# A routed filter-and-experts kernel: whole tiles of one pair of experts, and lists of single experts for the tokens left over

## The chip, the cores and the metric

The kernel runs on one core of one Trainium2 chip. A core has five engines that run side by side, each with its own queue of instructions, and wait for one another through semaphores: TensorE (PE, matrix products, whose loads of stationary operands are listed as PEld), VectorE (DVE), ScalarE (ACT), GpSimd (POOL) and SyncE (SP). Transfers between the chip's memory (DRAM) and the on-chip memory (SBUF) are issued by SP, ACT or POOL and carried out by 16 DMA engines. Products of PE land in PSUM, from where DVE or ACT read them.

The metric is the device time of one execution in microseconds. Differences of the median of several executions are looked at.

## The reference

The input is 16 x 1024 = 16384 tokens of 512 numbers (E = H = 512), with 8 experts, each a 512 x 512 matrix in float32. Every token goes to the two experts with the largest router probabilities.

```python
xn = _layernorm(x)
# s: a filter in frequency, then 24 bits per token, corrected, times W_le
x1 = ifft(fft(xn) * filt).real
bits = (sigmoid(x1 @ W_el + b_el) > 0.5)
s = x1 + _golay_correct(bits) @ W_le + b_le
# g: two of eight experts
probs = softmax(xn @ router_w.T)
topk_vals, topk_idx = top_k(probs, 2)
topk_w = topk_vals / (topk_vals.sum(-1) + 1e-6)
out = ((expert_out[topk_idx] + topk_vals) * topk_w).sum()   # over the two
g = silu(out)
return x + s * g
```

Here `expert_out` is `xn` times the matrix of each expert. The term `topk_vals` is a number per token and choice that is added to every element of that expert's result.

## The kernel before

A tile is 128 tokens; there are NT = 128 of them. The kernel has two passes, both with an order of instructions written out by hand (`tc.manual_schedule()`), so each engine runs its queue just as the Python loops emit it.

**Pass one** (`pass_1`) goes over the tokens in the order of memory. For each tile it computes the filter as matrix products and the logits of router and bits (`fold`, `transpose`, `filt`), stores the filtered values to DRAM (`yd`), and for rounds of tiles finds the two experts of every token (`route`). The two experts make one of 28 pairs. `scatter` writes the token's number into that pair's list in DRAM (`lists`), one indirect transfer of POOL per tile. `put_records` stores a record of 28 numbers per token (`recd`): in columns 0 to 7 the weights of the eight experts (six of them zero), in 9 the sum of weight times probability, in 10 and 11 mean and scale of the layer norm, and behind them the corrected bits.

At its end `bounds_a`, `bounds_b`, `place_q` and the four `takes` functions work out, from the counts of the pairs, where each of the 128 tiles of the second pass finds its tokens, and which experts it needs.

**Pass two** (from `mp = ctx.enter_context(...)`, L1026 on) goes over the tokens in the order of the lists. The pairs are put on a path (`pair_path`) on which neighbours share an expert, and the lists are read one behind the other along it, cut into 128 tiles with no regard to where a pair ends. A tile that lies in one pair needs two experts, and each of the 27 changes from pair to pair adds one more, so there are NI = 2 x 128 + 27 = 283 products of a tile with an expert. Which product belongs to which tile and expert depends on the data; it is read into registers (`load_regs`, L1110, four products at a time and four ahead), and the operands are addressed by these registers:

- `fetch_tok` (L1044) gathers 128 token numbers from the lists, `fetch_x` gathers their rows of x and their records, `fetch_y` their filtered values; `put` (L1186) scatters the results to the output. Every one of them is an indirect transfer of 128 rows, and all are issued on POOL's queue, in the order in which the loop calls them: five for each tile.
- `normalize` (DVE, L1079), `turn` (PE, L1087: four transposes into PSUM) and `enter` (ACT, L1093) bring a tile's normalized tokens, transposed, into a ring of 16 slots; `take` (ACT, L1124) copies the slot that a product needs.
- `product` (PE, L1135) multiplies with one expert: four steps over the inner size, eight instructions in the profile. DVE adds it, times the expert's column of weights, to the tile's sum (L1143). `open_tile` sets that sum to zero (L1099) and copies the eight weights (L1098).
- `triple`, `turn_code` (L1157, L1162, L1166) and `mend` (L1172, L1173) add the corrected bits' product to the filtered values; `gate` (ACT, L1150) is the silu; `combine` (DVE, L1177 to L1182) undoes the filter's halving, multiplies and adds x.

The loop runs over products `i`. Tile t = i / 2 is prefetched 8 (token numbers), 6 (x and records), 4 (normalized) and 2 (turned) tiles ahead, and is finished 14 tiles later, when all its products are sure to be done:

```python
for i in range(NI + 2 * LAST):
    t = i // 2
    f = t - LAST
...
    if i % 2 == 0:
        if 0 <= f - 1 < NT:
            put(f - 1)
        if t + AHEAD_R < NT:
            fetch_tok(t + AHEAD_R)
```

Five buffers of PSUM hold results of `product` and `mend`, two those of `turn`, one that of `turn_code`.

Of the kernel before, what the change touches and what calls it, by code (L numbers as in the profile page):

```python
# [21 lines left out]
RING = 16  # L22
# [5 lines left out]
def pair_path(ne=8):  # L28

    pairs = [(a, b) for a in range(ne) for b in range(a + 1, ne)]  # L30
    path, used = [(0, 1)], {(0, 1)}

    def go():
        if len(path) == len(pairs):
            return True
        for p in pairs:
            if p not in used and set(p) & set(path[-1]):
                path.append(p)
                used.add(p)
                if go():  # L40
                    return True
                path.pop()
                used.discard(p)
        return False

    assert go()
    return path
# [3 lines left out]
def kernel(  # L51
# [12 lines left out]
):  # L64

# [33 lines left out]
    NI = 2 * NT + NPAIR - 1  # L99
    NIP = (NI + 3) // 4 * 4  # L100

# [6 lines left out]
    yd = dram.tile([N, E], F32, name="yd")  # L108

# [21 lines left out]
    ones_b = p1c.tile([P, P], BF16, name="ones_b")  # L131
    iota_e = p1c.tile([P, NE], F32, name="iota_e")
# [3 lines left out]
    ord_sb = p1c.tile([NPAIR, 3 * NPAIR], F32, name="ord_sb")  # L136


    row_sb = p1c.tile([P, rows.shape[0]], F32, name="row_sb")
    base_r = row_sb[:, 0:NPAIR]  # L140
    dbase_r = row_sb[:, NPAIR : 2 * NPAIR]
    mem_r = row_sb[:, 2 * NPAIR : (2 + NE) * NPAIR].rearrange("p (e k) -> p e k", e=NE)
    at = (2 + NE) * NPAIR
    cnt_r = row_sb[:, at : at + 512]
    upto_r = row_sb[:, at + 512 : at + 512 + NE * NE].rearrange("p (a b) -> p a b", a=NE)
    bel_r = row_sb[:, at + 512 + NE * NE :]
# [66 lines left out]
    def constants():  # L213
# [19 lines left out]
        v.memset(wring, 0.0)  # L233
# [148 lines left out]
    def setup_code():  # L382
# [13 lines left out]
        for k in (1, 2):  # L396
# [15 lines left out]


            lambda: v.tensor_scalar(vi, vi, 16 * RING - 1, None, ALU.bitwise_and),
            lambda: v.tensor_scalar(ve, vi, -NONE, None, ALU.add),
# [22 lines left out]
    ti = mid.tile([P, 2], I32, name="ti")  # L438
    tf = mid.tile([P, 2], F32, name="tf")
    qi = mid.tile([P, NT], I32, name="qi")  # L440
    vi = mid.tile([P, NE], I32, name="vi")
    ve = mid.tile([P, NE], BF16, name="ve")
    NONE = 16.0 * ((NT - 1) % RING) + NE

# [198 lines left out]
    def route(n: int):  # L643
# [17 lines left out]
        def begin():  # L661
            s, j = t0 // GT, t0 % GT
            st.ex = (groups[s].wide if t0 < PAIRED else groups[s].ex)[:, j : j + S]
            st.rec = recs[(t0 // (2 * GT)) % 3][:, t0 % (2 * GT) : t0 % (2 * GT) + S, :]
            st.mx = new("mx", [P, S])
            v.tensor_reduce(st.mx, st.ex[:, :, L:X], AX.X, ALU.max)
# [11 lines left out]
        def largest(src, hot):  # L678
# [4 lines left out]
            def d():  # L683
                st.at = new("at", [P, S])
                v.tensor_reduce(st.at, st.eq, AX.X, ALU.max)
# [28 lines left out]
        def probs():  # L714
            st.sp = new("sp", SN)
            v.tensor_mul(st.sp, st.pb, st.sel)

        def norm_of():
            st.den = new("den", [P, S])
            v.tensor_reduce(st.den, st.sp, AX.X, ALU.add)  # L720

        ops += [chosen]
# [3 lines left out]
            lambda: v.tensor_mul(st.pb, st.pb, wide(st.sm)),  # L726
            probs,
            norm_of,
# [81 lines left out]
        def more():  # L810
            st.mo = small.tile([P, NPAIR], F32, name="mo", bufs=1)
            v.tensor_reduce(st.mo, st.q4.rearrange("p a k -> p k a"), AX.X, ALU.add)

        weights = [
            lambda: v.tensor_mul(st.rec[:, :, 0:NE], st.sp, wide(st.den)),
            lambda: v.tensor_mul(st.sp, st.sp, st.rec[:, :, 0:NE]),

            lambda: v.tensor_reduce(st.rec[:, :, 9], st.sp, AX.X, ALU.add),
# [17 lines left out]
    G = 16  # L836
    addrs = {}
    qf = bt.tile([P, NT], F32, name="qf")
    begin = bt.tile([P, NPAIR], F32, name="begin")
    step = bt.tile([P, NPAIR], F32, name="step")  # L840
    woff = bt.tile([1, NIP], I32, name="woff")
    slot = bt.tile([1, NIP], I32, name="slot")
    wcol = bt.tile([1, NIP], I32, name="wcol")
    wring = bt.tile([P, RING * 16], F32, name="wring")
    md = Group()

    def bounds_a():
        pc = ps_g.tile([P, 512], F32, name="pg")[0:NPAIR, 0:P]
        nc.tensor.matmul(pc, cum, ones_b, start=True, stop=True)
        md.cnt = mid.tile([NPAIR, P], F32, name="cntk")  # L850
        nc.vector.tensor_copy(md.cnt, pc)

    def bounds_b():

        po = ps_g.tile([P, 512], F32, name="pg")[:, 0 : 3 * NPAIR]
        nc.tensor.matmul(po, md.cnt, ord_sb, start=True, stop=True)
        nc.vector.tensor_copy(begin, po[:, 0:NPAIR])
        md.off = mid.tile([P, 2 * NPAIR], F32, name="off")
        nc.vector.tensor_copy(md.off, po[:, NPAIR:])
        nc.vector.tensor_sub(step, dbase_r, md.off[:, NPAIR:])  # L860

    def place_q(t: int, room):

        cmp = room[:, 0 : G * NPAIR].rearrange("p (g k) -> p g k", k=NPAIR)
        jump = room[:, G * NPAIR : G * (NPAIR + 1)]
        nc.vector.tensor_tensor(
            cmp,
            qf[:, t : t + G].unsqueeze(2).to_broadcast([P, G, NPAIR]),
            begin.unsqueeze(1).to_broadcast([P, G, NPAIR]),
            ALU.is_ge,  # L870
        )
        nc.vector.tensor_mul(cmp, cmp, step.unsqueeze(1).to_broadcast([P, G, NPAIR]))
        nc.vector.tensor_reduce(jump, cmp, AX.X, ALU.add)
        addrs[t // G] = bt.tile([P, G], I32, name="addr", bufs=2)
        nc.vector.tensor_add(addrs[t // G], jump, qf[:, t : t + G])

    def takes_a():

        end = md.off[:, 0:NPAIR]
        lo = mid.tile([P, NPAIR], F32, name="lo")  # L880
        nc.vector.tensor_scalar(lo, begin, tf[:, 0:1], None, ALU.max)
        hi = mid.tile([P, NPAIR], F32, name="hi")
        nc.vector.tensor_scalar(hi, end, tf[:, 1:2], None, ALU.min)
        nc.vector.tensor_tensor(lo, lo, hi, ALU.is_lt)
        use = mid.tile([P, NE, NPAIR], F32, name="use")
        nc.vector.tensor_mul(use, mem_r, lo.unsqueeze(1).to_broadcast([P, NE, NPAIR]))
        md.takes = mid.tile([P, NE], F32, name="takes")
        nc.vector.tensor_reduce(md.takes, use, AX.X, ALU.max)
        takes_b = mid.tile([P, NE], BF16, name="takes_b")
        nc.vector.tensor_copy(takes_b, md.takes)  # L890

        md.pn = ps_g.tile([P, 512], F32, name="pg")[:, 0:NE]
        nc.tensor.matmul(md.pn, tri_b, takes_b, start=True, stop=True)

    def takes_b():
        first = mid.tile([P, 1], F32, name="first")
        nc.vector.tensor_reduce(first, md.pn, AX.X, ALU.add)
        md.num = mid.tile([P, NE], F32, name="num")
        run = mid.tile([P, NE, NE], F32, name="run")
        nc.vector.tensor_mul(  # L900
            run, upto_r, md.takes.unsqueeze(1).to_broadcast([P, NE, NE])
        )
        nc.vector.tensor_reduce(md.num, run, AX.X, ALU.add)
        nc.vector.scalar_tensor_tensor(
            md.num, md.num, first, md.takes, ALU.add, ALU.mult
        )
        md.pi = ps_g.tile([P, 512], F32, name="pg")[0:1, 0:NIP]

    def takes_c(e: int):
        hot = mid.tile([P, NIP], BF16, name="hot", bufs=3)  # L910
        nc.vector.tensor_scalar(hot, cnt_r[:, 0:NIP], md.num[:, e : e + 1], None, ALU.is_equal)
        nc.tensor.matmul(md.pi, ve[:, e : e + 1], hot, start=(e == 0), stop=(e == NE - 1))

    def takes_d():
        nc.vector.tensor_scalar(wcol, md.pi, NONE, None, ALU.add)
        nc.vector.tensor_scalar(woff, wcol, NE - 1, None, ALU.bitwise_and)
        nc.vector.tensor_scalar(slot, wcol, 4, None, ALU.logical_shift_right)

    def pass_1():
# [23 lines left out]
        nc.gpsimd.iota(ti, pattern=[[P, 2]], base=0, channel_multiplier=P)  # L943
        nc.gpsimd.iota(vi, pattern=[[1, NE]], base=0, channel_multiplier=16)
        nc.gpsimd.iota(qi, pattern=[[P, NT]], base=0, channel_multiplier=1)
# [59 lines left out]
        bounds_a()  # L1005
        turn_a()
        bounds_b()
        turn_b()
        place_q(0, mid.tile([P, E], F32, name="cmp"))
        syndrome()  # L1010
        correct()
# [3 lines left out]
        takes_a()  # L1015
        takes_b()
        for e in range(NE):
            takes_c(e)
        takes_d()
# [6 lines left out]
    mp = ctx.enter_context(tc.tile_pool(name="mp", bufs=27))  # L1026
    xnp = ctx.enter_context(tc.tile_pool(name="xnp", bufs=3))
    xgp = ctx.enter_context(tc.tile_pool(name="xgp", bufs=22))
    w2 = ctx.enter_context(tc.tile_pool(name="w2", bufs=2))
# [73 lines left out]
    def load_regs(i: int):  # L1103
        for key, src, eng, top in (
# [12 lines left out]
            for n in range(4):  # L1117
                regs[key, i + n] = vals[n]
# [223 lines left out]
```

## Time and profile before

| | |
|---|---|
| median of 14 runs | 1552.24 us (1545.86 to 1562.89) |
| the profiled execution | 1555.33 us |
| its span | 1553.6 us |
| mean granted clock of PE | 0.962 |
| PE busy | 1425.9 us, 92% |
| DVE busy | 1144.2 us, 74% |
| POOL busy | 893.7 us, 58% |
| ACT busy | 627.3 us, 40% |
| instructions | 20646 |

The span is the time from the first to the last recorded instruction; the time of the execution holds a little more. The first pass takes some 370 us of it, the second the rest.

How to read the lines. A line of the page's groups gives the source line, the engine, the operation, what it writes and reads (`out<-in`), how often, and behind the bar the busy time in us, the mean of one in ns, and the idle time of the engine just before, with what ended it. In a line of the timeline come start and length in us, engine, line, operation, and in brackets the idle time before it and its releaser. "issue" means that the engine waited for nothing that the profile shows; "remote" or "an unknown queue" that a semaphore ended the wait for which the trace has no event in place. The ends of matmuls are modelled. In the slices each digit is the busy share of a fortieth of the span, in tenths.

### The profile page before, as it was taken

The numbers are of one execution on the slowest core, as the hardware profiler recorded it, in microseconds if no ns is written. First come the engines' busy times: TensorE is split into PE (matmuls) and PEld (weight loads), VectorE is DVE, ScalarE is ACT, GpSimd is POOL, SyncE is SP. The second block draws the span as 40 slices with busy tenths as digits, with TensorE's granted clock in tenths as the row PEclk, the third lists the DMA queues.
The fourth block names the chain that finished last, engine by engine and source line by source line (L and its number), as shares of the span: only waits on it lengthen the run. The fifth ranks groups of instructions, "written<-read, shape, count | busy, mean of one in ns | idle before, by whom it ended". The sixth has DMA issues, their size and how long they took to land.

```text
span 1553.6 us, 20646 instructions
## 1 busy us (share of the span) xinstructions
PE 1425.9 (92%) x5203; PEld 772.2 (50%) x5203; DVE 1144.2 (74%) x3043; ACT 627.3 (40%) x1346; POOL 893.7 (58%) x908
## 2 busy tenths in 40 slices
PE   3999999883999999898989889898999898999997
PEld 2888887672444444344434344344444343444443
DVE  7788888995343877777768677777787777779666
ACT  4988888761222332332323223233232323333221
POOL 1357777776544656666647456565756575564322
PEclk8999999995999999999999999999999999999999
DMA  6997766631111232233323222332333232232221
GB/s 230 318 333 259 223 224 224 161 100 52 51 43 54 94 97 90 91 96 104 99 81 107 80 90 90 96 98 90 110 97 97 90 111 90 90 97 96 76 74 61
DMA packets 91393, 185.07 MB, mean 119 GB/s; under 512 B 21998, under 2 KB 57710, under 8 KB 87182
## 3 DMA queue, kind: packets, MB, share of 16 engines
q0 software_dynamic: 43472, 104.51, 21.9%
q1 hardware_dynamic: 46702, 78.07, 15.0%
q10 hardware_dynamic: 1104, 1.17, 0.3%
q8 instruction: 46, 0.75, 0.2%
q14 instruction: 69, 0.57, 0.1%
HBM read 112.86 MB, written 70.84 MB: 118 GB/s over the span
## 4 chain that ended last, share of the span: by engine, by line
PE 56%; DVE 16%; issue 16%; another core or an unknown queue 5%; POOL 4%; ACT 1%; DMA 1%; DVEq 1%; POOLq 0%; ACTq 0%
PE pe L1135 36%; PE py L553 7%; PE pt L533 3%; PE pt L1087 2%; POOL yg L1044 2%; DVE aring L1143 2%; PE py L549 2%; PE py L550 1%; DVE mix L1181 1%; DVE yg L1173 1%; DVE aring L1099 1%; PE py L551 1%; PE pe L1172 1%; POOL rec L1044 1%
## 5 line engine op out<-in xcount | busy, mean ns | idle before, releaser
L1135 PE MATMUL pe<-w_sb,xw 128*128 x2264 | 1037.8, 608 | 3.1 <-issue 1.8
L1135 PEld LDWEIGHTS pe<-w_sb,xw 128*128 128x128 f32 x2264 | 419.9, 195 | 532.4 <-issue 509.8
L1143 DVE SCALAR_TENSOR_TENSOR aring<-pe,wring,aring 128x512 f32 x283 | 211.9, 749 | 275.9 <-remote 125.6
L1186 POOL DMA_INDIRECT out<-xg,tok x128 | 136.4, 1066 | 304.1 <-DVE xg L1182 195.2
L1150 ACT ACTIVATE aring<-aring,rec 128x512 f32<-128x512 f32 x128 | 92.4, 722 | 497.9 <-DVE aring L1143 378.5
L1124 ACT COPY xw<-xring 128x512 f32 x283 | 174.2, 617 | 29.1 <-PE pe L1135 21.5
L1044 POOL DMA_INDIRECT tok<-lists,at x120 | 124.7, 1039 | 88.1 <-DVE at L1060 55.4
L1044 POOL DMA_INDIRECT yg<-yd,tok x128 | 135.3, 1057 | 39.0 <-issue 39.0
L553 PE MATMUL py<-cm,pmt 128*128 128x288 f32 x512 | 157.6, 431 | 0.0
L799 POOL DMA_INDIRECT lists<-tok,dst x128 | 130.6, 1020 | 45.5 <-issue 22.8
L1044 POOL DMA_INDIRECT rec<-recd,tok x128 | 129.3, 1010 | 40.1 <-issue 34.2
L1044 POOL DMA_INDIRECT xg<-in_x,tok x128 | 128.9, 1007 | 40.6 <-issue 39.9
L526 POOL TENSOR_TENSOR mm<-xt 128x256 f32<-128x256 f32 x128 | 97.8, 764 | 91.7 <-PE pt L533 65.1
L1093 ACT COPY xring<-pt 128x512 f32<-128x512 f32 x128 | 73.0, 570 | 104.6 <-PE pt L1087 61.7
L556 ACT ACTIVATE yb<-py,rec 128x576 f32<-128x576 f32 x128 | 94.8, 741 | 48.0 <-PE py L553 35.8
L1166 ACT CAST ct<-pc 96x128 bf16<-96x128 f32 x128 | 32.9, 257 | 198.1 <-remote 96.2
L1181 DVE TENSOR_TENSOR mix<-mix,aring 128x512 f32<-128x512 f32 x128 | 88.6, 692 | 14.7 <-ACT xw L1124 0.9
L553 PEld LDWEIGHTS py<-cm,pmt 128*128 128x128 f32 x512 | 88.6, 193 | 13.8
L1087 PEld LDWEIGHTS pt<-ident,xn 128*128 128x128 f32 x512 | 64.7, 142 | 59.7 <-issue 45.4
L486 ACT ACTIVATE no<-xt,sum 128x512 bf16<-128x512 f32 x128 | 91.0, 712 | 3.7 <-DVE pp L466 2.1
L1182 DVE TENSOR_TENSOR xg<-mix,xg 128x512 f32<-128x512 f32 x128 | 88.8, 694 | 4.4
L1173 DVE TENSOR_TENSOR yg<-pe,yg 128x512 f32<-128x512 f32 x128 | 87.2, 682 | 1.7 <-issue 0.6
(227 smaller groups left out, 1628.8 us busy)
## 6 DMA issues: line engine op xcount, KB each, us to landing
xt<-in_x SPq DMA_DIRECT2D x32, 1024.0 KB
yd<-yb SPq DMA_DIRECT2D x32, 1024.0 KB
w_sb<-in_expert_w SPq DMA_DIRECT2D x8, 1024.0 KB
lists<-tok,dst POOLq DMA_INDIRECT x128
xg<-in_x,tok POOLq DMA_INDIRECT x128
rec<-recd,tok POOLq DMA_INDIRECT x128
yg<-yd,tok POOLq DMA_INDIRECT x128
out<-xg,tok POOLq DMA_INDIRECT x128
```

The lines of the kernel that those rows point to most:

```text
L526: nc.gpsimd.tensor_tensor(m, xr[:, 0:H], xr[:, H:E], ALU.subtract)
L553: nc.tensor.matmul(py[:, 1, 0 : X + H], pmt[:, 2 + c, :], cm[:, c, :], start=(c == 0), stop=(c == 1))
L556: nc.scalar.activation(y_room(g), py[:, :, 0:WY], AF.Copy, scale=k.rec[:, j, 11:12])
L799: dma = nc.gpsimd.indirect_dma_start(out=lists, out_offset=bass.IndirectOffsetOnAxis(ap=st.dst[:, j : j + 1], axis=0), in_=tok[:, t0 + j : ...
L1044: nc.gpsimd.indirect_dma_start(out=dst, out_offset=None, in_=src, in_offset=bass.IndirectOffsetOnAxis(ap=idx, axis=0), bounds_check=limit - 1,
L1087: nc.tensor.transpose(k.pt[:, c * P : (c + 1) * P], k.xn[:, c * P : (c + 1) * P], ident)
L1124: nc.scalar.copy(xw.rearrange("p c t -> p (c t)").unsqueeze(1), xring[:, bass.ds(regs.pop(("a", i)), 1), :],)
L1135: nc.tensor.matmul(pe.unsqueeze(1), xw[:, c, :], w_sb[:, bass.ds(e, 1), c, :], start=(c == 0), stop=(c == KC - 1),)
L1143: nc.vector.scalar_tensor_tensor(acc, pe.unsqueeze(1), wring[:, bass.ds(regs.pop(("c", i)), 1)], acc, ALU.mult, ALU.add,)
L1173: nc.vector.tensor_add(k.y, pw, k.y)
L1181: nc.vector.tensor_mul(mix, mix, aring[:, t % RING, :])
L1186: dma = nc.gpsimd.indirect_dma_start(out=of, out_offset=bass.IndirectOffsetOnAxis(ap=k.tok, axis=0), in_=k.x, in_offset=None, bounds_check ...
```

## The change

The second pass is written anew, and the end of pass one with it.

- Each pair's list is cut into whole tiles of 128 tokens. There are at least NPURE = 101 of these over all pairs, and 101 are used. A whole tile needs just two experts, the same for all its tokens.
- What is left over (27 tiles of tokens, NREST, of any pair) is handled as 61 *items* (NITEM): lists of 128 tokens that all go to one expert, two of whose entries come from each token left over. An item multiplies x with its expert and stores the product to DRAM (`ed`). Later 27 *rest* tiles gather, for their 128 tokens, the two products from `ed`, and finish as a whole tile does.
- The record holds two weights, in columns 0 and 1, for the lower and the higher expert of the pair, in place of eight. `route` computes them on arrays of one number per token.
- At the end of pass one, `whole_a`, `whole_b` and `whole_c` work out the whole tiles, gather all their token numbers by one transfer and transpose them on PE; `rest_a`, `rest_b` and `rest_c` prepare the addresses of items and rest tiles, which `item_adr`, `item_experts` and `rest_adr` complete on DVE beside the first 16 tiles (`side`).
- The rings, `enter`, `take`, `open_tile` and the look-ahead of the register loads are gone. The loop runs over tiles; x is turned two tiles ahead into one of four buffers, the first product is scaled on ACT and the second added to it on DVE, and a tile is combined and put at the start of the next one.
- The order is fixed: 12 whole tiles; 61 items with 29 whole tiles spread among them; 6 whole tiles; 27 times rest, whole, whole.

The core of the diff (the tables of constants on the host, and the parts of the functions not named below, are left out):

```diff
+    NREST = NPAIR - 1
+    NPURE = NT - NREST
+    NITEM = 2 * NREST + NE - 1
...
         weights = [
-            lambda: v.tensor_mul(st.rec[:, :, 0:NE], st.sp, wide(st.den)),
-            lambda: v.tensor_mul(st.sp, st.sp, st.rec[:, :, 0:NE]),
-            lambda: v.tensor_reduce(st.rec[:, :, 9], st.sp, AX.X, ALU.add),
+            weigh,
+            biases,
+            lambda: v.tensor_add(st.rec[:, :, 9], st.sm, st.p2),
+            swap,
+            lambda: v.tensor_mul(st.lo, st.lo, st.den),
+            lambda: v.tensor_add(st.rec[:, :, 0], st.w2, st.lo),
+            lambda: v.tensor_sub(st.rec[:, :, 1], st.w1, st.lo),
         ]
...
+    def whole_b():
...
+        nc.gpsimd.indirect_dma_start(
+            out=md.tt[0:NPURE, :],
+            out_offset=None,
+            in_=lists.rearrange("(r c) o -> r (c o)", c=P),
+            in_offset=bass.IndirectOffsetOnAxis(ap=idx[0:NPURE, :], axis=0),
...
+    def whole_c():
+        tf_ = mid.tile([P, P], F32, name="ttf")
+        nc.vector.tensor_copy(tf_[0:NPURE, :], md.tt[0:NPURE, :])
+        pt = ps_g.tile([P, 512], F32, name="pg")[:, 0:NPURE]
+        nc.tensor.transpose(pt, tf_[0:NPURE, :], ident[0:NPURE, 0:NPURE])
+        nc.vector.tensor_copy(toks, pt)
...
+    AHEAD_K, AHEAD_X, AHEAD_Y, AHEAD_N, AHEAD_T = 7, 5, 2, 3, 2
...
+    def fetch_tok(k):
+        if k.kind == "whole":
+            k.tok = toks[:, k.n : k.n + 1]
+            return
+        k.tok = mp.tile([P, 1], I32, name="tok2")
+        adr = adr_i if k.kind == "item" else adr_r[:, 0, :]
+        gather(k.tok, lists, adr[:, k.n : k.n + 1], NPAIR * N)
...
+    def fetch_y(k):
+        if k.kind == "item":
+            return
+        k.y = w2.tile([P, E], F32, name="yg", bufs=4)
+        gather(k.y, yd, k.tok, N)
+        if k.kind == "rest":
+            k.parts = []
+            for h in range(2):
+                part = w2.tile([P, E], F32, name=f"part{h}", bufs=2)
+                gather(part, ed, adr_r[:, 1 + h, k.n : k.n + 1], NITEM * P)
+                k.parts.append(part)
...
+    def turn(k):
+        if k.kind == "rest":
+            return
+        pt = ps_x.tile([P, KC * P], F32, name="pt2")
+        for c in range(KC):
+            nc.tensor.transpose(pt[:, c * P : (c + 1) * P], k.xn[:, c * P : (c + 1) * P], ident)
+        k.xt = w2.tile([P, KC, P], F32, name="xt2", bufs=4)
+        nc.scalar.copy(k.xt.rearrange("p c t -> p (c t)"), pt)
...
+    def expert(k, h: int):
+        src, i = (woff, h * P + k.n) if k.kind == "whole" else (ioff, k.n)
+        if (src is woff, i) not in regs:
+            load_regs(src, i)
+        return regs.pop((src is woff, i))
...
+    def scaled(out, src, k):
+        nc.scalar.activation(out, src, AF.Copy, scale=k.rec[:, 0:1])
+
+    def added(k, src):
+        nc.vector.scalar_tensor_tensor(k.acc, src, k.rec[:, 1:2], k.acc, ALU.mult, ALU.add)
+        nc.scalar.activation(k.acc, k.acc, AF.Silu, bias=k.rec[:, 9:10])
+
+    def work_on(k, beside):
+        if k.kind == "item":
+            pe = product(k, 0)
+            beside()
+            res = w2.tile([P, E], F32, name="res", bufs=3)
+            nc.scalar.copy(res, pe)
+            nc.sync.dma_start(out=ed[k.n * P : (k.n + 1) * P, :], in_=res)
+            return
+        k.acc = w2.tile([P, E], F32, name="acc", bufs=3)
+        if k.kind == "whole":
+            pe = product(k, 0)
+            scaled(k.acc, pe, k)
+            beside()
+            mend(k)
+            added(k, product(k, 1))
+        else:
+            beside()
+            mend(k)
+            scaled(k.acc, k.parts[0], k)
+            added(k, k.parts[1])
...
+    LEAD, PAUSE = 12, 6
+    TAIL = 2 * NREST
+    kinds = ["whole"] * LEAD
+    among = NPURE - LEAD - PAUSE - TAIL
+    for j in range(NITEM):
+        kinds += ["item"]
+        kinds += ["whole"] * ((j + 1) * among // NITEM - j * among // NITEM)
+    kinds += ["whole"] * PAUSE + ["rest", "whole", "whole"] * NREST
...
+        for n in range(-AHEAD_K, NTILE + 2):
+            each(n + AHEAD_K, fetch_tok)
+            each(n + AHEAD_X, fetch_x)
+            each(n + AHEAD_Y, fetch_y)
+            each(n - 1, combine)
+            each(n - 1, put)
+            each(n + AHEAD_N, normalize)
+            each(n + 2, triple)
+
+            def beside():
+                each(n + AHEAD_T, turn)
+                each(n + 1, turn_code)
+
+            if 0 <= n < NTILE:
+                work_on(tiles[n], beside)
+            else:
+                beside()
+            if n >= 0 and side:
+                side.pop(0)()
```

`mend` now also holds the four operations of DVE that undo the halving (L1177 to L1180 before), and `combine` the last two alone.

## The prediction

> **What bounds the kernel now.** I read four views in this order: the page's slices and groups, the windows by stage, the timeline of one tile, and the timeline around a stop together with the waits.
>
> ```profile
> PE   3999999883999999898989889898999898999997
> POOL 1357777776544656666647456565756575564322
> ...
> L1186 POOL DMA_INDIRECT out<-xg,tok x128 | 136.4, 1066 | 304.1 <-DVE xg L1182 195.2
> ...
> L1044 POOL DMA_INDIRECT yg<-yd,tok x128 | 135.3, 1057 | 39.0 <-issue 39.0
> ...
> L1044 POOL DMA_INDIRECT xg<-in_x,tok x128 | 128.9, 1007 | 40.6 <-issue 39.9
> ```
>
> The second pass is slices 10 to 40. PE is nearly full there; POOL shows 5 to 6 tenths, but each of its transfers also has a gap of 0.30 us ("issue") before it, so an issue occupies it for 1.34 us (mean of the five kinds 1.04, plus 0.30).
>
> ```profile
> 420.00:490.00 70.00, 70.00 (x193) 32.78 (x192) 28.39 (x63) 17.01 (x28) 30.21 (x30) 1.00 0.16 41
> 509.00:549.00 40.00, 40.00 (x115) 18.64 (x114) 31.86 (x73) 13.66 (x27) 26.89 (x26) 1.00 0.33 101
> ...
> 800.00:1000.00 200.00, 183.26 (x510) 84.65 (x509) 142.23 (x324) 56.82 (x112) 121.28 (x118) 0.97 0.31 95
> ```
>
> The columns are time, then busy time and count of PE, PEld, DVE, ACT, POOL, then clock, DMA share, GB/s. At 509 to 549 POOL issues 26 transfers in 40 us (1.53 us each) and PE is full. At 800 to 1000 it issues 118 in 200 us (1.69 each), yet PE loses 17 us and its clock is 0.97.
>
> ```profile
> 747.25 0.22 PE L1162 MATMUL pc<-ident_b,b 128*96 128x128 bf16 x1
> 747.30 3.65 PE L1135 MATMUL pe<-w_sb,xw 128*128 x8
> 750.79 0.38 PE L1172 MATMUL pe<-wle,ct 96*128 96x512 bf16 x1
> 751.01 0.60 PE L1087 MATMUL pt<-ident,xn 128*128 128x128 f32 x4
> 751.45 3.60 PE L1135 MATMUL pe<-w_sb,xw 128*128 x8
> 754.89 0.22 PE L1162 MATMUL pc<-ident_b,b 128*96 128x128 bf16 x1
> ```
>
> From start to start one undisturbed tile costs PE 7.64 us: two products of 3.46, the turn of x 0.44, the code's turn 0.05 and its product 0.22.
>
> ```profile
> 1200.61 0.60 PE L1087 MATMUL pt<-ident,xn 128*128 128x128 f32 x4
> 1202.43 1.02 POOL L1186 DMA_INDIRECT out<-xg,tok  x1 [0.31 <-issue]
> 1207.70 1.01 POOL L1044 DMA_INDIRECT yg<-yd,tok  x1 [0.30 <-issue]
> 1210.73 0.75 DVE L1143 SCALAR_TENSOR_TENSOR aring<-pe,wring,aring 128x512 f32 x1 [8.23 <-remote]
> 1211.07 0.26 PE L1162 MATMUL pc<-ident_b,b 128*96 128x128 bf16 x1 [6.42 <-ACT ct L1166]
> ```
>
> ```profile
> POOL out L1186 <- DVE xg L1182: 129.1, 25, 8.9
> ...
> DVE aring L1143 <- remote: 119.3, 22, 8.5
> ```
>
> This is the loss. POOL had issued back to back since 1181.9; DVE and ACT stood in waits on PE's semaphore whose matmuls the records show long done, and got on 2 us after POOL's last issue (1208.7). From 500 to 1450 us 22 such waits took 119 us. Between them POOL runs 15 to 24 issues (20 to 34 us), then mostly pauses 6 to 9 us, waiting for DVE's result before `put`. What holds the semaphore the trace does not say; it goes with POOL running without gaps.
>
> **The change, part by part.** The sum is against the profiled execution (1555.33 us, span 1553.6), 3.1 above the median 1552.24.
>
> *Products and turns.* 283 products become 202 for 101 whole tiles and 61 for the items: 20 fewer, 20 x 3.46 = 69 us off PE. Turns rise from 128 to 162: 34 x 0.44 = 15 us. PE's second pass by undisturbed rows: before 128 x 7.64 + 27 x 3.46 = 1071 us; after 101 x 7.64 + 61 x 3.90 + 27 x 0.27 = 1017 us. A saving of 54 us if PE is what ends.
>
> *ACT and DVE.* 283 copies at L1124 (617 ns), 128 memsets (485 ns), the copy at L1098 and 155 accumulations at L1143 (749 ns) go; ACT gets 128 scalings and 61 copies of some 0.6 us. Both were off the path except in the waits above: nothing. Per whole tile DVE keeps 0.54 + 0.19 + 0.68 + 1.43 + 0.75 + 1.39 = 5.0 us; `side` adds four operations (3 x 0.62 + 0.17, the rows of L866 to L875) to each of the first 16 tiles, 7.0 of 7.64 us: hidden by the products, at most 5 us.
>
> *New waits.* `combine` now stands at the head of the next tile on DVE and waits for the silu (0.72 us at L1150 and the handoffs, about 0.9); `normalize` three tiles ahead, `triple` and `mend` queue behind it. 5.0 + 0.9 is still under 7.64, so nobody waits for those. Without that cover it would cost 0.9 us a tile. SP, which issues nothing after 375 us before, gets 61 stores of an item's product, 256 KB each: hidden, for the parts that read them are gathered at least six tiles (46 us) after the last.
>
> *Pass one and the seam.* The weights become about seven more but smaller DVE operations (0.18 against 0.22 to 0.75) under a full PE; at the very end they delay the last record by 1.4 us. The list gather with its transpose takes the place of the first `tok` gather (373.02 to 376.05), while the nine `takes` groups (L881 to L917, 374.95 to 381.9) leave DVE. First product at 386.7 as before; bounds -3 and +4.
>
> *PE's register loads.* `expert` loads four registers right before the product that needs them, in place of four products ahead. A load takes 333 ns on PE's queue and the next register operation came 0.43 us after its start. 40 loads lie in PE-bound stretches; 0 to 0.5 us each, I take 8 us.
>
> *POOL.* This is the part that costs. Per tile before: tok, x, rec, y, put = 5. After: whole tile 4, item 3, rest tile 7 (tok, x, rec, y, two parts, put). The order is 12 whole; 61 items among 29 whole; 6 whole; then 27 times rest, whole, whole. By group:
> - 12 whole: POOL 5.3 of PE's 7.64 us. 92 us, plus 9 for the start, which the old kernel also lost (first 12 tiles took 96.3, 88 at its pace then of 7.3).
> - items: PE 61 x 3.90 + 29 x 7.64 = 460 us; POOL 299 issues, 1.54 us each at that pace, like the 1.53 of 509 to 549. Lower bound 460 (no loss, as there), upper 502 (x 8.33/7.64, the mean tile of 600 to 1400: 473 issues in 800 us, five a tile). Middle: 481.
> - 6 whole: 47 us.
> - tail: a group needs 15 issues but only 2 x 7.64 + 0.27 + pc = 15.6 us of PE. Issues made ahead (tok 7 tiles, x and rec 5, y 2) leave 389. The bounds: 1.34 each, never a pause, 521 us; 1.69, with the pauses of 600 to 1400, 657 us. A POOL that must issue all the time has more cause for holds than that stretch, but `put` comes a tile later than y asks for it, which gives slack. I take the middle, 1.52: 591 us.
> - after the last issue 5 us (1548.66 to 1553.6).
>
> Sum: 386.7 + 101 + 481 + 47 + 591 + 8 + 5 = 1620 us of span; +1.7 outside, -3.1 to the median: **1618 us**, 4% slower.
>
> The Trainium skill speaks against my main term: "DMA: Bandwidth & Descriptors", section "Anatomy of one DMA — SWDGE (gpsimd) path", puts the two microseconds of a transfer mostly into waiting for the write's receipt and calls descriptor generation small. By it POOL could issue ahead and PE would set the end, 1430 us. The rows above differ: 1.0 us of POOL and 0.3 of gap per transfer, of 128 rows each, whatever its bytes; the trace decides.
>
> **The rivals.** *No holds (faster).* POOL runs through the tail without a pause and the items cost PE's own time: 386.7 + 101 + 460 + 46 + 521 + 4 + 5 = 1524, 1522 by the median. For it: 26 issues in 40 us at 509 without loss, and more slack before `put`. Against: no later run of back-to-back issues passed 35 us. The tail turns the sign: under 1.36 us an issue (items at 481) the kernel gains.
>
> *Holds everywhere (slower still).* The items look ahead only two tiles of 3.9 us, 7.8 us, where the old products had two of 7.64; a semaphore late by 8 us now stops PE each time. Items at 1.69 x 299 = 505 plus 20 of stops, tail 657, 15 for registers: 386.7 + 101 + 525 + 48 + 657 + 15 + 5 = 1738, 1736 by the median. Against: fewer PSUM buffers are waiting per item.
>
> *PE bound throughout.* 386.7 + 9 + 1017 + 8 + 10 = 1431. It needs 15 issues in 15.6 us, 1.04 each; the shortest spacing in the trace is 1.28. That the products don't fall is excluded, the lists are fixed in length.
>
> A slow clock changes nothing: the product after PE's stop before 861.6 took 6.21 us in place of 3.65 (granted clock 0.5 there), but even 27 dips that cost 3.4 us each leave the tail's PE work at 27 x 19 = 513 us, under POOL's 521.
>
> **How the numbers follow.** Forecast (tail at 1.42 to 1.62 an issue) 0.55; no holds 0.23, a quarter of it within 0.3%, which is what can be told from no change here; holds everywhere 0.20; PE bound 0.02. The time is the forecast's. The range cuts 1 in 10 off at each side: 1530 to 1715. Faster 0.19, same 0.06, slower 0.75.
>
> **What would show it.** POOL solid at 8 to 9 tenths in the last 600 us with PE at 6 to 7; issues 1.4 to 1.6 us apart there; DVE waiting for y or a part; "remote" waits in the items; 1052 x 2 product matmuls at the old 608 ns. If PE is full in the tail, or POOL's issues lie under 1.3 us apart, I am wrong.

## The result, and the profile after

| | before | after |
|---|---|---|
| median | 1552.06 us (47 runs, 1538.83 to 1565.77) | 1658.97 us (10 runs, 1644.76 to 1677.02) |
| ratio | | 1.0683 (95%: 1.0650 to 1.0716) |
| span of the profiled execution | 1553.6 us | 1647.8 us |
| granted clock of PE, mean | 0.962 | 0.934 |
| PE busy | 1425.9 us | 1393.3 us |
| POOL busy | 893.7 us, 908 instructions | 1048.2 us, 1045 instructions |

The kernel became 6.8% slower. The prediction was 1618 us, slower, with a range of 1530 to 1715. The ratio is of the runs that lie within 1.5% of the fastest of their kernel.

The slices and the groups of the kernel after, as they were shown of the kernel before:

```profile
PE   3999999857999899899999999677876676777676
POOL 1367777865766666566656666766766676676663
...
L1180 PE MATMUL pe<-w_sb,xt 128*128 x2104 | 972.4, 612 | 0.5 <-ACT xt L1155 0.5
...
L1256 POOL DMA_INDIRECT out<-xg,toks x101 | 106.7, 1056 | 228.0 <-DVE xg L1251 154.9
...
L1105 POOL DMA_INDIRECT xg<-in_x,toks x101 | 106.7, 1056 | 36.4 <-issue 30.6
L1105 POOL DMA_INDIRECT yg<-yd,toks x101 | 107.8, 1067 | 30.8 <-issue 30.8
```

PE is as full as before up to slice 25 and then falls to 6 to 8 tenths; POOL stands at 6 or 7 there. The products are down from 2264 instructions to 2104 at the same length (612 against 608 ns): the work that was to go went. `put` waits for DVE as before.

The second pass as one window, before and then after (columns: time, busy time and count of PE, PEld, DVE, ACT, POOL, then granted clock, DMA share, GB/s):

```profile
387.00:1550.00 1163.00, 1100.11 (x3024) 507.36 (x3023) 817.35 (x1835) 342.58 (x665) 652.78 (x631) 0.97 0.29 88
```

```profile
391.00:1637.00 1246.00, 1064.17 (x3001) 509.86 (x2999) 637.60 (x1367) 311.21 (x606) 806.43 (x769) 0.93 0.38 120
```

PE's busy time fell by 36 us; the time in which PE stood still rose from 63 to 182 us. POOL's work rose by 154 us. Where PE stands still the windows by stage of the kernel after show (items, and then the tail of rest, whole, whole):

```profile
485.00:973.00 488.00, 466.98 (x1374) 226.73 (x1373) 176.26 (x371) 124.92 (x239) 305.43 (x299) 0.99 0.38 117
...
1018.00:1637.00 619.00, 459.32 (x1236) 216.94 (x1234) 361.26 (x780) 149.35 (x295) 409.56 (x387) 0.88 0.39 124
```

Of PE's 182 idle microseconds 160 lie in the tail and 21 beside the items. In the tail POOL issues 386 transfers in 618 us, 1.60 us each. Between two pauses of over 5 us they come in runs of 24 to 37, once of 60, at 1.38 us from start to start. There are 11 such pauses, 73 us together. One of them, in the timeline of the kernel after from 1238 us on, so that of the first product only the end is shown (start, length, engine, line, operation, idle time before and its releaser):

```profile
1237.53 1.45 PE L1180 MATMUL pe<-w_sb,xt 128*128 x3
...
1242.68 0.75 DVE L1222 SCALAR_TENSOR_TENSOR acc<-pe,rec,acc 128x512 f32<-128x512 f32 x1 [5.01 <-remote]
...
1246.15 1.12 PE L1153 MATMUL pt<-ident,xn 128*128 128x128 f32 x4 [7.17 <-DVE xn L1144]
...
1249.95 1.01 POOL L1105 DMA_INDIRECT yg<-yd,toks  x1 [0.30 <-issue]
...
1251.98 0.69 DVE L1211 TENSOR_TENSOR yg<-pe,yg 128x512 f32<-128x512 f32 x1 [5.78 <-remote]
...
1252.75 5.04 PE L1180 MATMUL pe<-w_sb,xt 128*128 x8
...
1257.27 1.02 POOL L1256 DMA_INDIRECT out<-xg,toks  x1 [6.31 <-DVE b L1195]
```

By the records PE's products ended at 1239.0. DVE got at one of them only at 1242.68; by the order of the instructions, the product that it took there had ended at 1230.1. Then it waited 5.78 us, until 1251.98, for PE's result at L1210, whose last record before that ended at 1235.5; POOL had begun its last issue 2 us before. Then everything runs on, but POOL stays without work until DVE has brought `put` its tile. I call this whole event a stop. The waits of the tail, by the list of waits (total, times, longest):

```profile
ACT acc L1219 <- remote: 68.5, 12, 7.8
...
POOL out L1256 <- DVE b L1195: 55.8, 13, 7.6
DVE yg L1211 <- remote: 55.5, 8, 9.2
...
POOL out L1256 <- DVE xg L1251: 40.0, 9, 6.2
```

They are the pair that was shown of the kernel before, ACT and DVE behind PE's semaphore and POOL behind DVE.

### The profile page after: what moved, and what is told of

It reads as the page before. It is cut to its first block, busy times and chain, and to the rows that moved or that the text cites. A ratio compares the mean times of both kernels' runs of the same rounds, so it can differ in the third digit from the quotient of the medians.

```text
span 1647.8 us, 19181 instructions
## 1 busy us (share of the span) xinstructions
PE 1393.3 (85%) x5189; PEld 777.6 (47%) x5189; DVE 962.9 (58%) x2642; ACT 595.6 (36%) x1297; POOL 1048.2 (64%) x1045
## 4 chain that ended last, share of the span: by engine, by line
PE 59%; DVE 16%; another core or an unknown queue 9%; issue 9%; ACT 3%; POOL 1%; DMA 1%; POOLq 0%; DVEq 0%; ACTq 0%
PE pe L1180 39%; PE py L539 6%; PE pt L1153 4%; PE pt L519 3%; DVE acc L1222 2%; DVE mix L1250 2%; PE py L535 2%; DVE yg L1211 2%; ACT acc L1223 2%; PE pe L1210 1%; PE py L536 1%; DVE mix L1215 1%; DVE xn L1144 1%; PE py L537 1%
## 5 line engine op out<-in xcount | busy, mean ns | idle before, releaser
L1180 PE MATMUL pe<-w_sb,xt 128*128 x2104 | 972.4, 612 | 0.5 <-ACT xt L1155 0.5
L1180 PEld LDWEIGHTS pe<-w_sb,xt 128*128 128x128 f32 x2104 | 409.6, 197 | 440.8 <-issue 435.1
L1223 ACT ACTIVATE acc<-acc,rec 128x512 f32<-128x512 f32 x128 | 92.4, 722 | 518.2 <-DVE acc L1222 377.2
L1256 POOL DMA_INDIRECT out<-xg,toks x101 | 106.7, 1056 | 228.0 <-DVE xg L1251 154.9
L1155 ACT COPY xt<-pt 128x512 f32<-128x512 f32 x162 | 93.7, 578 | 221.5 <-remote 65.5
L787 POOL DMA_INDIRECT lists<-tok,dst x128 | 130.6, 1020 | 45.8 <-issue 22.3
L1153 PE MATMUL pt<-ident,xn 128*128 128x128 f32 x648 | 103.0, 284 | 65.4 <-DVE xn L1144 60.8
L1105 POOL DMA_INDIRECT xg<-in_x,toks x101 | 106.7, 1056 | 36.4 <-issue 30.6
L1105 POOL DMA_INDIRECT yg<-yd,toks x101 | 107.8, 1067 | 30.8 <-issue 30.8
L1105 POOL DMA_INDIRECT rec<-recd,toks x101 | 106.9, 1058 | 30.8 <-issue 30.5
L1144 DVE TENSOR_SCALAR xn<-xg,rec 128x512 f32<-128x512 f32 x162 | 89.0, 560 | 23.0 <-DMA rec<-recd,toks 14.5
```

Source lines behind the costliest of these rows:

```text
L787: dma = nc.gpsimd.indirect_dma_start(out=lists, out_offset=bass.IndirectOffsetOnAxis(ap=st.dst[:, j : j + 1], axis=0), in_=tok[:, t0 + j : ...
L1105: nc.gpsimd.indirect_dma_start(out=dst, out_offset=None, in_=src, in_offset=bass.IndirectOffsetOnAxis(ap=idx, axis=0), bounds_check=limit - 1,
L1144: nc.vector.tensor_scalar(k.xn, k.x, k.rec[:, 10:11], k.rec[:, 11:12], ALU.subtract, ALU.mult)
L1153: nc.tensor.transpose(pt[:, c * P : (c + 1) * P], k.xn[:, c * P : (c + 1) * P], ident)
L1180: nc.tensor.matmul(pe.unsqueeze(1), k.xt[:, c, :], w_sb[:, bass.ds(e, 1), c, :], start=(c == 0), stop=(c == KC - 1),)
L1223: nc.scalar.activation(k.acc, k.acc, AF.Silu, bias=k.rec[:, 9:10])
```

## The experiments

The runs came in six sets, each on one chip, with the kernel before beside them there. That kernel took 1470 us in four of the sets (each on another chip), 1550 in one and 1528 in one. Absolute times are therefore compared only within a set; a ratio is always against the kernel before of the same set. "A chip with stops" or "without" means in what follows that the traces taken there show such long waits marked "remote", or show none. Each of these chips was used in one set only, so that the chip can't be told from the time at which it was used.

### Put two tiles later (e1_put_late)

```diff
-        for n in range(-AHEAD_K, NTILE + 2):
+        for n in range(-AHEAD_K, NTILE + 4):
...
-            each(n - 1, put)
+            each(n - 3, put)
```

Two more buffers for x go with it.

> Only the place of the output transfers on POOL's queue is changed: put comes two tiles later, so that POOL may issue two tiles further before it has to wait for DVE. Theory A1 (PE's semaphores come late by at most some 14 us while POOL issues back to back, and the pauses are only POOL meeting put too early): the pauses of 5 to 7.5 us in the tail go, 386 issues at 1.36 us in place of 1.60, about 93 us less, 1565 us. Theory A2 (the semaphores stay late for as long as POOL issues without a pause): the runs grow longer, but end in the same pauses, 0 to 25 us less, 1635 to 1660 us. Theory B (the tail waits for the bytes of its transfers): no change.

Measured: 1533.66 us beside 1470.15 of the kernel before, ratio 1.0434 (1.0413 to 1.0455). The tail's window of this kernel:

```profile
986.00:1519.00 533.00, 451.54 (x1237) 208.58 (x1234) 364.21 (x776) 146.12 (x295) 413.77 (x383) 0.95 0.46 143
```

POOL runs through the tail in a single run of 383 issues, 1.39 us each, and there is no wait marked "remote" in it. No figure that had been expected was this low. The chip differed too: the kernel before took 82 us less here than in the first comparison, presumably without its own stops (no trace of it at 1470 us was taken). So the run alone doesn't say whether `put`'s place or the chip took the pauses away. It does say that the tail without a pause still costs 533 us while PE works 452 of it: the bound looks like POOL's number of issues, which the next two runs test.

### The parts read by SP (e2_parts_sp)

The two products of a rest tile are read as plain rows of `ed`, by SP, in place of two gathers by address on POOL; these are other rows than the tile's own, so the kernel leaves out the lookup of a token's two products.

```diff
-                gather(part, ed, adr_r[:, 1 + h, k.n : k.n + 1], NITEM * P)
+                i = 2 * k.n + h
+                nc.sync.dma_start(out=part, in_=ed[i * P : (i + 1) * P, :])
```

> The two products of a rest tile are read as whole rows of the store by SP, in place of two gathers on POOL; the same bytes, but other rows than the rest tiles need. Theory A (the tail costs its issues on POOL, 1.60 us each): 54 issues fewer, 86 us less, about 1573 us. Theory B (the tail waits for bytes and for the arrival of its transfers): the bytes are the same, no change within 10 us. Theory C (the tail is set by PE's stops on late semaphores and the short look-ahead, whatever POOL does): no change or a little.

Measured: 1470.93 us, ratio 1.0003 (0.9992 to 1.0013). The tail's window:

```profile
990.00:1458.00 468.00, 425.97 (x1236) 198.00 (x1233) 362.13 (x778) 143.64 (x295) 356.30 (x334) 1.00 0.52 162
```

The tail made 333 issues in 467.6 us, 1.40 each, against 383 in 533.0 at 1.39 with put two tiles later, the nearest run on this chip (the kernel after itself was not run there). 50 issues fewer gave 65 us: 1.31 us for each issue that went, with the bytes still read. That the tail waits for its bytes doesn't fit this. And here `put` stands where the change had put it, yet 331 issues run without a pause. Its early place alone doesn't make the pauses.

### Filtered values and record by one transfer (e3_merged)

Pass one stores both into rows of 540 numbers (`yr`); whole and rest tiles gather such a row in place of two. Items still gather the record alone.

```diff
-        k.rec = mp.tile([P, META], F32, name="rec")
-        gather(k.rec, recd, k.tok, N)
...
+        both = xgp.tile([P, E + META], F32, name="yr")
+        gather(both, yr, k.tok, N)
+        k.y = both[:, 0:E]
+        k.rec = both[:, E:]
```

> Record and filtered values of a token lie in one row of 540 numbers, so that a whole tile and a rest tile gather them with one transfer in place of two. 128 issues fewer on POOL, the same bytes. Theory A: the tail loses 81 of its 386 issues at 1.60 us, 130 us; the items section comes nearer to PE's own 460 us, 10 to 20 less: about 1515 us, below the kernel before. Theory B: no change within 10 us. Theory C: up to 30 us less.

Measured: 1450.27 us, ratio 0.9866 (0.9847 to 0.9886), with the whole computation. The tail's window:

```profile
1000.00:1439.00 439.00, 422.92 (x1231) 198.17 (x1229) 355.84 (x776) 143.78 (x295) 332.63 (x307) 1.00 0.55 172
```

The tail fell to 439.7 us with 307 issues (1.43 each), and PE was busy 423 of them, almost its own bound. The first product came at 402.8, some 12 us later than in the kernel after, after pass one with its additional stores; which of them delays it wasn't tried.

### The same, with three whole tiles to a rest tile (e4_merged_order)

```diff
-    LEAD, PAUSE = 12, 6
-    TAIL = 2 * NREST
+    LEAD, PAUSE = 8, 5
+    TAIL = 3 * NREST
...
-    kinds += ["whole"] * PAUSE + ["rest", "whole", "whole"] * NREST
+    kinds += ["whole"] * PAUSE + ["rest", "whole", "whole", "whole"] * NREST
```

> As the merged rows, and the order changed: 8 whole tiles, the 61 items with only 7 whole tiles among them, 5 whole tiles, then 27 times rest and three whole tiles. Every stretch then has about 1.55 us of PE work for each POOL issue. Theory A: start 391, 8 tiles 66, items 61 x 4.8 + 7 x 4.8 = 326 (POOL), 5 tiles 38, tail 405 issues at 1.57 = 636, end 11: 1468 us, some 5% below the kernel before. If pauses vanish at that pace, 1440. Theory C (PE's stops on late semaphores decide): 1540 or more.

Measured: 1424.95 us, ratio 0.9693 (0.9677 to 0.9709), faster than both kernels. Slices and a window of it:

```profile
PE   2999999989289999999999999999999999999997
...
POOL 1346777777565777777763676767676767767661
```

```profile
500.00:1400.00 900.00, 900.00 (x2685) 438.87 (x2684) 557.56 (x1198) 276.31 (x551) 616.96 (x580) 1.00 0.49 152
```

PE is full for 900 us on end at a granted clock of 1.00; POOL shows 3 to 4 tenths idle, but its 580 issues at 1.39 us from start to start take 806 of the 900 us, so it has one tenth to spare. The second pass takes 1010 us from first to last product (403.5 to 1413.3), where the prediction's count of PE's work gave 1017.

### Both kernels again (j1_after, j2_before)

> The changed kernel again, unchanged, beside the kernel before, to see how much of its loss rests on the stops. In the comparison at the head of the document both kernels lost time in stops in which DVE and ACT waited for PE's semaphore and POOL for DVE; in the first four experiments the kernel before took 1470 us and no such stop was seen. Theory (POOL's issues bound the tail, stops are an extra): where no stops occur, the tail costs 386 issues x 1.39 us = 537 in place of 618 us, the items 458 in place of 487, so 391 + 92 + 458 + 46 + 537 + 8 = 1532 us of span, 1.04 times the kernel before; where stops occur, 1640 to 1680 and 1.065 to 1.072. Rival (the wait of DVE for y and the parts, which put asks for one tile too late, makes the pauses by itself): 1640 or more in either case, since put is one tile late here whatever the stops do; with 1470 before that is a ratio of 1.11.

Measured: 1665.37 us beside 1550.44, ratio 1.0718 (1.0630 to 1.0807). This chip had the stops: the tail took 618.1 us, the items 506.3, the lead 94.7. The theory's figures for such a chip hold; the rival's 1640 or more isn't excluded by this run.

> The kernel before, unchanged, for its trace where it takes 1470 us. Theory (its second pass is PE's work plus stops that come while POOL issues without a gap): at 1470 us its runs of POOL issues end in no pause of 6 to 9 us for DVE, no wait of DVE or ACT on PE's semaphore over 5 us is left from 500 to 1450 us (22 with 119 us in the first profile), and PE is busy in over 97% of the second pass. Rival (the granted clock makes the difference of 82 us): the waits and pauses are there as before, and the mean product matmul is 5% shorter.

Measured: one run, 1564.68 us, with 23 waits of DVE at L1143 on PE's semaphore (137.8 us) from 500 to 1450. So it showed the stops a second time and no trace at 1470 us; what it was sent for stayed open. Its rival, the granted clock, is too small by an estimate from the clocks on record: the mean clock of the kernel before was 0.981 to 0.985 in the sets at 1470 us and 0.961 to 0.969 in this one. A difference of 2.4% at most of a span of some 1550 us is under 40 us, about half of what separates the sets.

### A pause in POOL's queue (g1_breathe, m1_breathe)

```diff
+    def breathe():
+        a = w2.tile([P, 1], F32, name="ba", bufs=1)
+        nc.gpsimd.memset(a, 0.0)
+        b = w2.tile([P, 1], F32, name="bb", bufs=1)
+        nc.sync.dma_start(out=b, in_=a)
+        nc.gpsimd.memset(b, 0.0)
...
+            if i % 6 == 0:
+                breathe()
             if i % 2 == 0:
                 if 0 <= f - 1 < NT:
                     put(f - 1)
```

> The kernel before with a pause put into POOL's queue once in three tiles (ahead of put): POOL writes a small tile, SP copies it to another by a DMA, and POOL waits for that, some 2 to 2.5 us in which POOL issues nothing. Theory (PE's semaphore updates come late while POOL issues without a gap, and come in some 2 us after its last issue): on a chip where the kernel before takes 1550 us and shows the stops, runs of issues are now cut to 15 (20 us), the waits of 5 us and more on PE's semaphore go, and the time falls to 1470 to 1500 (POOL needs 15 x 1.34 + 2.5 = 22.6 of PE's 22.9 us, so the pause itself just fits). Rival (stops come from something else and POOL's pauses are only their effect): the pauses take POOL's spare time away and the kernel is 0 to 40 us slower. On a chip where the kernel before takes 1470 us both say 1470 to 1480.

Measured: 1496.82 us beside 1470.41, ratio 1.0175 (1.0158 to 1.0192). The chip had no stops, so the run doesn't tell the theories apart. It shows a price, in the list of waits of this kernel from 500 to 1450 us:

```profile
POOL bb L1189 <- DMA bb<-ba: 107.8, 40, 4.1
```

40 waits of 2.7 us for a tiny transfer, 3.6 us (median) of pause in POOL's issuing with what lies around each, and the time was not the 1470 to 1480 expected. Three tiles' issues (15 in 20.1 us) and the pause make 23.7 us against PE's 22.9: taking 2.5 us for the pause was the error. It also shows how near POOL's bound the kernel before already was.

> The kernel before with the pause in POOL's queue once in three tiles, again; where the kernel before took 1470 us this took 1497, so the pauses cost 27 us by themselves. On a chip with stops (kernel before at 1525 to 1555): theory (PE's semaphore updates come late while POOL issues without a gap, and a gap of 3.6 us lets them in): 1497 to 1505 again, faster than the kernel before there by 30 to 50 us, and no wait of DVE on PE's semaphore over 5 us is left. Rival (the stops come from something else): 1550 to 1580, slower than the kernel before by some 27 us, with the waits as before. On a chip without stops: 1497, tells nothing.

Measured: 1495.31 us beside 1470.44, ratio 1.0171 (1.0136 to 1.0207): again a chip without stops, and nothing on the theories.

### Put later and the merged version again (g2_put_late, g3_merged_order, n1_merged_order)

> The changed kernel with put two tiles later, which took 1533 us (1.043 of the kernel before) on a chip without stops. On a chip with stops (kernel before at 1550): theory 1 (stops end only when POOL pauses, and it pauses when put finds DVE late): the runs of issues in the tail grow by the 10 issues of two tiles, from some 32 to 42, and one pause of 7 us comes per 42 issues in place of 32: 386 x 1.39 + 9 x 7 = 600 in place of 618, total 1640 to 1650. Theory 2 (put came too early by itself, and that alone made the pauses): the pauses go, 1545 to 1565. On a chip without stops: 1533 again.

> The changed kernel with the filtered values and the record gathered by one transfer for whole and rest tiles, and with three whole tiles to each rest tile in the tail (8 whole tiles ahead, 5 between). It took 1425 us, 0.969 of the kernel before, on a chip without stops. On a chip with stops (kernel before at 1550): if stops come with POOL issuing without a gap, they are fewer, since each group of a rest and three whole tiles needs 15 issues x 1.39 = 20.9 of PE's 23.2 us and leaves POOL a gap of 2.3 us: 1425 to 1450, ratio 0.92 to 0.935. If they come with the number of transfers whatever the gaps, the loss is that of the kernel before, 80 us: 1505, ratio 0.97. On a chip without stops: 1425 again.

> The version with the merged transfer and three whole tiles to each rest tile, again, for a chip with stops: it took 1425 us, 0.969 of the kernel before, where the kernel before took 1470. Theory (stops come while POOL issues without a gap; here 2.4 us of gap follow each 15 issues in the tail): 1425 to 1450 where the kernel before takes 1525 to 1555, ratio 0.92 to 0.945. Rival (stops come with the number of transfers, gaps or not): 1480 to 1510, ratio 0.965 to 0.975, and waits of DVE on PE's semaphore over 5 us through the tail. On a chip without stops: 1425, ratio 0.969.

Measured: put later 1535.63 us, ratio 1.0446 (1.0425 to 1.0467); the merged version 1424.19, ratio 0.9690 (0.9674 to 0.9706), and on a further chip 1423.07, ratio 0.9676 (0.9660 to 0.9693). Both chips gave 1470 us for the kernel before, so the figures expected for chips without stops came (1533, 1425), and those for chips with stops weren't put to the test.

### The kernel after, a third time (k1_after)

> The changed kernel, unchanged, for the case of a chip on which the kernel before takes 1470 us. Theory (POOL's issues bound the tail, the stops are an extra of the chip): 391 + 92 + 458 + 46 + 386 x 1.39 + 8 = 1532 us of span, as with put two tiles later, ratio 1.043, and one long run of issues in the tail. Rival (put asks one tile too early, whatever the chip): pauses of some 7 us after each 24 to 36 issues in the tail here too, 1610 or more, ratio 1.09 and up. On a chip with the kernel before at 1550: 1640 to 1680 again.

Measured: 1636.04 us beside 1528.17, ratio 1.0706 (1.0536 to 1.0877), on a chip between the two others. The tail took 596.8 us, and from 1156 on its issues came in runs of 45 (62 us, so 1.38 us each) with pauses of 5.5 to 7.6 us between. The same instructions thus stopped after 24 to 60 issues on one chip and mostly after 45 on another; that isn't set by `put`'s place alone either.

## Why the prediction was right, and where its sizes were off

Stretches of the second pass, read from the starts of the product matmuls at L1180, in us:

| stretch | predicted | kernel after | put later, chip without stops |
|---|---|---|---|
| until the first product | 386.7 | 391.0 | 391.2 |
| 12 whole tiles | 101 | 94.5 | 91.9 |
| 61 items, 29 whole tiles | 481 (+8 for registers) | 487.2 | 457.6 |
| 6 whole tiles | 47 | 45.8 | 45.8 |
| tail | 591 | 618.2 | 533.0 |
| behind | 5 | 11.1 | 11.8 |
| span | 1620 | 1647.8 | 1531.2 |

*POOL sets the end of the tail: right, and shown.* Fewer issues shortened the tail in proportion (383, 333, 307 issues in 533, 468, 440 us), until PE's own work was reached. "DMA: Bandwidth & Descriptors" of the Trainium skill, section "Anatomy of one DMA — SWDGE (gpsimd) path", which calls descriptor generation small, had been set against this; the runs side with the rows, at 1.38 to 1.40 us of POOL for each issue of 128 rows.

*The tail's size: 27 us short.* The prediction had 521 us of bare issues and took 70 more for pauses. Measured were 386 x 1.38 = 533 of issues, 73 in the 11 long pauses, and 12 for shorter ones and the run-out, in which the last tiles follow each other some 5 to 7 us apart. So the size of the pauses fits, but by luck: the 70 us were the middle between no pause and the pace of 600 to 1400 us, and on other chips the pauses of over 5 us came to 70 us, to 52 us or to none. The bare issue was 1.38 us where the rows of before gave 1.34 (their means of 1007 to 1066 ns are 1014 to 1067 here), and the run-out had no term. The ground given for the middle, that a POOL that must issue all the time has more cause for holds, was not borne out: 11 pauses over 5 us in 618 us here, 23 in 950 us (500 to 1450) before.

*The seam: 4.3 us late, just past the upper bound of 4.* The list gather and its transpose were put in place of the first gather of token numbers, 373.02 to 376.05, with no price of their own. The timeline there:

```profile
374.54 2.28 POOL L885 DMA_INDIRECT tt<-lists,idx  x1 [2.58 <-DVE sm L661]
...
380.68 0.23 DVE L906 CAST ttf<-tt 101x128 f32<-101x128 int32 x1 [3.91 <-DMA tt<-lists,idx]
...
382.63 1.05 POOL L1105 DMA_INDIRECT xg<-in_x,toks  x1 [5.81 <-DVE toks L909]
...
390.95 3.73 PE L1180 MATMUL pe<-w_sb,xt 128*128 x4
```

It held POOL for 2.28 us and landed about 6 us after its start; the first row of x was asked for at 382.63, where the kernel before did it at 376.05. 

*Items: right to 2 us, by luck.* 487.2 against 489, with the registers' 8. Where there are no stops, this stretch costs 457.6, under the prediction's lower bound of 460, and PE is full, as the window of put later shows:

```profile
483.00:941.00 458.00, 458.00 (x1373) 224.44 (x1372) 176.10 (x370) 125.03 (x239) 301.86 (x295) 1.00 0.40 124
```

Register loads cost nothing that shows there, so the term of 8 us was wrong, and the whole excess is stops; on the two other chips with stops the stretch took 492.7 and 506.3. The upper bound of 502 was also misworked: 473 issues in 800 us at five a tile are 8.46 us a tile and not 8.33, which makes it 509 and the middle 485. The lead was 6 us shorter, the end behind the last product 6 us longer than the terms had them.

*PE's saving: right, and not received.* The prediction counted 54 us less of PE's work. The merged version in the new order got 45 of them (1470.15 to 1424.95), in spite of a first product 12 us later.

*The rival "no holds": the mechanism exists, its sign was wrong.* It gave 1524 us of span and called that faster. On chips without stops the span was 1531 with put later, but the kernel before takes 1470 there (the prediction's own PE count gives 386.7 + 9 + 1071 = 1467 for it). The step that failed is the comparison of an undisturbed kernel after with a disturbed kernel before. "Faster below 1.36 us an issue" falls with it: at 1.39 the ratio is 1.043, and equal time needs the 50 issues fewer of the SP reading.

*Signs that did not come.* POOL in the tail was not solid at 8 to 9 tenths but read 6 to 7, as the gap of 0.3 us in each issue doesn't count as busy and the pauses come on top. DVE's long waits there were marked "remote", for PE's results, and not for y or a part; waits for those showed on a chip without stops, with put later (33.6 us of DVE for y, 57.7 us of ACT for the parts).

*What the stops are: open.* That they go with POOL issuing without a gap was argued from the traces of chips that have them. Issuing without a gap is not enough by itself: with put later POOL made 383 issues on end and no stop came. Whether gaps prevent them was not shown, as both runs with the pause fell on chips without stops. Not run were the kernel after unchanged on a chip without stops, and the merged version on a chip with them.

## What to carry to other kernels

Count the issues of each queue for each stage against the bottleneck engine's time in that stage, not over the span: here POOL was busy for 58% of the span before, and 15 issues at 1.38 us in a group with 15.6 us of PE cost more than all that was saved on PE. When small transfers are issue-bound, merge rows that share an index before reordering work, then spread the costly tiles until the stage fits. And price a rival that removes a disturbance on both sides of the comparison.

## What the runs showed of the hardware

- The kernel before took 1470 us on four chips (within 1468 to 1472), 1528 on one and 1550 on one; the last has a profile there, and it shows the stops. The five traces taken where the kernel before took 1528 us or more have 22 to 36 waits of DVE or ACT marked "remote" of over 4 us each between 420 and 1400 us; the nine traces taken where it took 1470 us have none. On the chip of 1528 the kernel after stopped after 45 issues. Without stops POOL made 383 issues in one run.
- The time of one issue in an unbroken run didn't differ by chip: 1.38 to 1.40 us.
- For the same products of the tail the granted clock was 1.00 where PE stood still for 9% of it (SP reading, PE busy 426 us), 0.95 at 15% (put later, 452 us) and 0.88 at 26% (kernel after, 459 us). None of it set the time, since POOL did.
- A transfer of a [128, 1] tile from SBUF to SBUF kept POOL waiting 2.7 us (mean of 40), and its pause in issuing was 3.6 us (median).
